# A second table stored by rank from SP's queue, with each node's place carried in the first table

## The chip, the cores and the metric

The kernel runs on one core of a Trainium2 chip. A core has five engines that run at once, each on its own in-order stream: TensorE (PE, matrix products; PEld is its loading of weights), VectorE (DVE), ScalarE (ACT), GpSimd (POOL) and SyncE (SP). Sixteen DMA engines move data between memory and the core's buffers; transfers are issued from the queues of SP, ACT or POOL. The metric is device time of one execution in microseconds, the median of several runs.

## The reference

Two layers of a typed graph transformer over 6250 nodes with 128 features and 100,000 edges, 8 heads of 16 numbers. A node has one of 16 types, an edge one of 32.

```
k, q, v = typed_linear(x, ntype, Wk / Wq / Wv)      # one 128x128 matrix per node type
kT = einsum('nhd,htdo->nhto', k, Watt)              # for every node, all 32 edge types
vT = einsum('nhd,htdo->nhto', v, Wmsg)
kw, m = kT[src, :, etype], vT[src, :, etype]        # one row per edge
a   = einsum('ehd,ehd->eh', kw, q[dst]) * pri[:, etype].T / 4
att = edge_softmax(a, dst)                          # over the edges of one dst
hag = segment_sum(m * att, dst)
h   = silu(typed_linear(hag, ntype, Wa))
h   = h * alpha + x * (1 - alpha)                   # alpha = sigmoid(skip[ntype])
out = layernorm(h) * g + b
```

After two such layers a last linear map is added to the input x and the sum is normalized.

## The kernel before, in words

The kernel forms kT and vT for every node and edge type as a table in device memory: one row of 256 numbers (128 of kT with the softmax scale, 128 of vT) for each pair of node and edge type, 1 KB, about 205 MB per layer. Row number is node × 32 + edge type. An edge then costs one gathered row.

**Ranks.** The nodes are sorted by class of type (four classes of four types) and by degree into 50 blocks of 128; a node's place in this order is its rank, 128 × block + partition. The blocks' numbers of edge slots are fixed ahead (`KB`, 8 to 41, 867 slots in all). `rank_order` (L644 to L927) finds the ranks on VectorE and TensorE: `degrees` compares all destinations with 64 values (L537), then come a histogram (L672 to L686) and a loop over superblocks (L781 to L798) that ends in `rank` at L807. From the ranks it makes lists by place: `start` (first edge), `degr`, `node` and `row2` (the row numbers of a node's table halves, L851). Then it yields "gathers" and issues, on POOL, the gathers of each block's edge list into `ell` (L869: one number node × 32 + edge type for every edge slot) and of its rows of x (L881). `rank_order` is a generator: the table's loop pulls it step by step.

**First table** (L1011 to L1028). It is made in order of type: `inv` says which node stands at each place, `fetch` (L943) gathers its row of x on POOL, `linears0` makes k and v of a window of types, and `table_block` (L287) multiplies each block of 128 nodes by the block matrices of the edge weights, for 16 edge types at a time (`tg` 0 and 1): eight products, copied from PSUM into a tile `st` of 128 × 16 × 256 numbers by ScalarE (L306) or VectorE (L304). `put0` (L1001) scatters `st` into the table on POOL's queue: 16 KB per partition, at the row that `rows1` names. Four `st` tiles exist. 98 such stores make the table; `stage` decides how many steps of ranking go beside each half.

**First edge pass** (`edges(0)`, L1103). The 50 blocks are taken in 15 superblocks of three or four. For each edge slot POOL gathers 128 rows (L1274), one for each node of the block, by the column of `ell`, into a ring `kvr` of 50 slots. For every six to eight slots VectorE multiplies the first half of the rows by q (L1286) and sums by head (L1290); when a block is complete, `finished` computes its softmax (exp on ScalarE, L1170), weighs the second halves (L1189) and adds them up (L1200, L1205), which frees the slots. A slot is gathered into again only when its block's sums are done.

**Nodes and second table.** When a superblock is complete, `nodes` (L1357) computes Wa, the skip, the norm and the next layer's k, v and q; `pieces_of` (L1478) makes the second table from k and v by `table_block` with three `st` tiles, and `scatter` (L1483) stores each tile, three steps late, on POOL's queue, to the row that `row2` names: 100 such stores, between the gathers. The second table thus has the same row numbers as the first, and `ell` serves both passes. Its first gather waits for all of these stores (L1277 to L1284).

**Second edge pass.** It is the same loop over the second table; `nodes` ends in the output rows, scattered on POOL (L1517).

**What orders the work.** POOL's instructions are in the order in which the program writes them (a manual schedule). Those of the other engines are ordered by a planner that models their times and takes what is ready in the order of the program. `tick` and `spread` decide how many steps of `nodes` and `pieces_of` are written for each edge slot. SP's queue carries the loads of rows by rank (`hr`, L1074), of types (`ntb`, L1066) and of q (L1099), and the stores of `hrd` (L1401) and `qrd` (L1452); each waits in order until its buffer is free or its data is there.

Of the kernel before, what the change touches and what calls it, by code (L numbers as in the profile page):

```python
# [18 lines left out]
P = 128  # L19
# [100 lines left out]
def kernel(  # L120
# [60 lines left out]
    tabs = [dram.tile([NP * RT, 2 * D], F32, name=f"tab{l}") for l in range(L)]  # L181
    kvs = dram.tile([PAD, 1], I32, name="kvs")
# [104 lines left out]
    def table_block(pool, ps_pool, kT, vT, i, share, bufs, store, w=1):  # L287


        for tg in range(TG):  # L290
            tt = slice(tg * 16, (tg + 1) * 16)
            st = pool.tile([P, 16, 2 * D], F32, name="st", bufs=bufs)
            for half, (yT, bd) in enumerate(((kT, bdk), (vT, bdv))):
                for hp in range(0, HP, w):
                    pt = ps_pool.tile([P, w, SB * P], F32, name="tb").rearrange(
                        "p b (t c) -> p b t c", t=16)
                    for b in range(w):
                        s = slice((hp + b) * 2 * HS, (hp + b + 1) * 2 * HS)
                        nc.tensor.matmul(pt[:, b], yT[s, i * P:(i + 1) * P], bd[s, tt, :],  # L299
                                         start=True, stop=True)  # L300
                    c0 = half * D + hp * 2 * HS
                    to = st[:, :, c0:c0 + w * 2 * HS].rearrange("p t (b c) -> p b t c", b=w)
                    if hp in share:
                        nc.vector.tensor_copy(to, pt)  # L304
                    else:
                        nc.scalar.copy(to, pt)  # L306
                yield
            store(tg, st)
# [333 lines left out]
    with tc.manual_schedule(engines={mybir.EngineType.Pool}):  # L642

        def rank_order():  # L644
# [162 lines left out]
            nc.vector.tensor_tensor(rank, rank, none, op=ALU.add)  # L807
            ranki = pp.tile([P, NT], I32, name="ranki")
# [202 lines left out]
        got, stage = [], ""  # L1011
        for _ in linears0(got, 0):
            pass
        for t in range(TY):
            b0, _, b1 = spans(t)
            beside = linears0(got, t + 1) if t + 1 < TY else iter(())
            for b in range(b0, b1):
                def store(tg, st, b=b):
                    put0(st, tg, b)
                    fetch(min(b + AHEAD, fetched[0] + 1))  # L1020
                share = (1,) if stage in ("gathers", "done") else ()
                for half, _ in enumerate(table_block(tp, tnb, *got[t], b - b0, share, STB0, store)):
# [11 lines left out]
    def arm(fast):  # L1034
# [9 lines left out]
        if fast:  # L1044
            kvr = npl.tile([P, SLOTS, 2 * D], F32, name="kv")
# [57 lines left out]
        def edges(l):  # L1103
# [50 lines left out]
            def finished(s, i, chunks, kvt, used, a, pair, sums, den):  # L1154
# [74 lines left out]
            for s, (i0, k, types) in enumerate(sbs):  # L1229
# [6 lines left out]
                for i in range(k):  # L1236
# [24 lines left out]
                    for j0, j1 in chunks:  # L1261
# [10 lines left out]
                        for j in range(j0, j1):  # L1272
                            at = KO[b] + j
                            get = nc.gpsimd.indirect_dma_start(  # L1274
                                out=kv[:, j - j0, :], out_offset=None, in_=tabs[l][:],
                                in_offset=bass.IndirectOffsetOnAxis(ap=ell[:, at:at + 1], axis=0))
# [10 lines left out]
                            kk, kk, q.unsqueeze(1).to_broadcast([P, c, D]), op=ALU.mult)  # L1287
                        for r in range(c):
# [189 lines left out]
        def pieces_of(i0, k, kT, vT, share):  # L1478
# [4 lines left out]
            def scatter(tg, st, b):  # L1483
                put = nc.gpsimd.indirect_dma_start(  # L1484
# [200 lines left out]
```

## Time and profile before

| | |
|---|---|
| median of 3 runs | 3683.18 us (3673.71 to 3688.72) |
| profiled execution | 3703.66 us, span 3701.5 us |
| busy: PE, DVE, ACT, POOL | 1811.8, 1953.0, 1018.8, 2150.0 us |
| granted clock of PE, mean | 0.641 |
| moved | 691.11 MB, mean 187 GB/s |

| stage | us from the start |
|---|---|
| loads and order by type | 0 to 61 |
| first table | 61 to 656 |
| first edge pass, nodes, second table | 656 to 2306 |
| second edge pass, output | 2306 to 3701 |

A page of the profile shows the busy time of each engine, the span in 40 slices (each digit a busy share in tenths), the DMA queues, and groups of instructions by line: busy time and mean duration in ns, and after the bar the time for which the engine stood idle just before them, with what ended the waits. A line Lnnn is a line of the kernel. The engine of a wait is the one that waited; behind the arrow stands what it waited for. "Issue" is time in which nothing was waited for that the profile shows.

### The profile page before, as it was taken

The page shows a single profiled execution, that of the slowest core. Times are in us where ns is not written, and L with a number is a line of the kernel's source. Part 1 is how long each engine was busy: PE and PEld are TensorE (multiplying, and loading weights), DVE is VectorE, ACT ScalarE, POOL GpSimd, SP SyncE. Part 2 cuts the span into 40 slices and gives each one's busy share as a digit, 9 for nine tenths or more (in the row PEclk, how much of TensorE's full clock was granted, in tenths as well). Part 3 has the DMA queues.
Part 4 walks back from the last instruction along what each step waited for, and adds up shares of the span by engine and source line. Part 5 has one row for each costly group of instructions (what it writes and reads, how often), then busy time and mean ns, then how long its engine had stood idle before and what let it go on. Part 6 is the DMA issues. An engine that isn't in the chain of part 4 may idle for free. (4 is left out here: it accounts for less than half of the span.)

```text
span 3701.5 us, 22085 instructions
## 1 busy us (share of the span) xinstructions
PE 1811.8 (49%) x5612; PEld 822.8 (22%) x5612; DVE 1953.0 (53%) x4025; ACT 1018.8 (28%) x1677; POOL 2150.0 (58%) x2213
## 2 busy tenths in 40 slices
PE   3898998115555687658677675002120122112112
PEld 1344445002222232222222222001010111101011
DVE  8665231356355665457456633445655447455645
ACT  2675565002331244213332353001100111011111
POOL 2224663674676566666665652765667566666653
PEclk9789675557666776667678677555555555555555
DMA  6797999634655477546764677333333333333321
GB/s 181 309 385 319 399 403 403 161 99 147 218 188 195 140 269 268 176 148 210 268 220 165 241 284 304 107 96 91 95 92 107 86 89 102 92 99 94 91 82 43
DMA packets 194484, 691.11 MB, mean 187 GB/s; under 512 B 55469, under 2 KB 106032, under 8 KB 169298
## 3 DMA queue, kind: packets, MB, share of 16 engines
q0 software_dynamic: 119120, 651.15, 49.7%
q1 hardware_dynamic: 58838, 31.29, 3.2%
q10 hardware_dynamic: 16384, 7.11, 0.9%
q8 instruction: 48, 0.79, 0.1%
q14 instruction: 94, 0.77, 0.1%
HBM read 264.91 MB, written 429.48 MB: 188 GB/s over the span
## 5 line engine op out<-in xcount | busy, mean ns | idle before, releaser
L1274 POOL DMA_INDIRECT kv<-tab,ell x1734 | 1722.7, 993 | 769.2 <-issue 481.5
L306 ACT COPY st<-tb 128x512 f32<-128x512 f32 (+1 forms) x1064 | 726.1, 756 | 510.5 <-PE tb L299 255.0
L284 PE MATMUL nb<-ident,hag 128*128 128x128 f32 x100 | 26.1, 400 | 743.9 <-issue 212.5
L299 PE MATMUL tb<-bdv,kvT 32*128 32x512 f32 x800 | 275.7, 834 | 77.2 <-ACT st L306 66.2
L1484 POOL DMA_INDIRECT tab<-st,row x100 | 106.5, 1065 | 345.3 <-ACT st L306 288.5
L299 PE MATMUL tb<-bdv,vT 32*128 32x512 f32 x784 | 291.9, 868 | 24.4 <-ACT st L306 14.2
L299 PE MATMUL tb<-bdk,kvT 32*128 32x512 f32 x800 | 267.7, 824 | 67.5 <-ACT st L306 60.6
L1286 DVE TENSOR_TENSOR kv<-kv,q 128x896 f32<-128x896 f32 (+4 forms) x135 | 136.3, 1011 | 288.8 <-DMA kv<-tab,ell 260.4
L1290 DVE TENSOR_REDUCE a<-kv 128x48 f32<-128x768 f32 (+4 forms) x269 | 269.8, 1004 | 32.7 <-remote 23.2
L278 PE MATMUL nb<-xm,wa 128*128 128x384 f32 (+1 forms) x384 | 228.9, 758 | 117.5 <-DVE xm L269 79.3
L269 DVE SCALAR_TENSOR_TENSOR xm<-ntb,nb 128x384 f32<-128x384 bf16 (+1 forms) x336 | 184.4, 592 | 169.3 <-PE nb L284 50.6
L299 PE MATMUL tb<-bdk,kT 32*128 32x512 f32 x784 | 257.2, 865 | 0.9 <-issue 0.8
L1002 POOL DMA_INDIRECT tab<-st,rows x98 | 103.7, 1058 | 240.2 <-ACT st L306 195.1
L1286 DVE TENSOR_TENSOR kv<-kv,tb 128x768 f32<-128x768 f32 (+4 forms) x134 | 135.2, 1010 | 157.7 <-DMA kv<-tab,ell 130.7
L284 PE MATMUL nb<-ident,hs 128*128 128x128 f32 x100 | 37.8, 460 | 367.1 <-DVE hs L1395 165.1
L304 DVE COPY st<-tb 128x512 f32<-128x512 f32 (+1 forms) x120 | 89.1, 744 | 199.8 <-PE tb L299 141.1
L284 PEld LDWEIGHTS nb<-ident,hag 128*128 128x128 f32 x100 | 15.9, 198 | 762.5 <-issue 726.1
L278 PE MATMUL nb<-xm,wq 128*128 128x384 f32 (+1 forms) x192 | 106.7, 721 | 118.3 <-DVE m L1165 80.9
L1417 PE MATMUL nb<-xm,wkqv 128*128 128x384 f32 (+1 forms) x288 | 133.3, 617 | 51.0 <-DVE xm L269 32.6
L1200 DVE TENSOR_TENSOR tb<-kv,tb 128x512 f32<-128x512 f32 (+3 forms) x211 | 121.2, 574 | 69.5 <-remote 46.7
L278 PEld LDWEIGHTS nb<-xm,wa 128*128 128x128 f32 x384 | 98.7, 274 | 244.3 <-issue 113.4
L1436 PE MATMUL nb<-xm,wkqv 128*128 128x384 f32 (+1 forms) x288 | 132.3, 619 | 11.6 <-DVE xm L269 9.8
(314 smaller groups left out, 2745.4 us busy)
## 6 DMA issues: line engine op xcount, KB each, us to landing
kv<-tab,ell POOLq DMA_INDIRECT x1734
hr<-xrd SPq DMA_DIRECT2D x30, 192.0 KB
hr<-xrd SPq DMA_DIRECT2D x15, 256.0 KB
xrd<-xr POOLq DMA_DIRECT2D x11, 256.0 KB
ntb<-typed SPq DMA_DIRECT2D x20, 96.0 KB
hrd<-hs SPq DMA_DIRECT2D x10, 192.0 KB
qrd<-q SPq DMA_DIRECT2D x10, 192.0 KB
q<-qrd SPq DMA_DIRECT2D x10, 192.0 KB
```

Of the source, the lines that this page charges most:

```text
L269: nc.vector.scalar_tensor_tensor(xm[:, :n], ntb[:, :n], float(t), hT[:, :n], op0=ALU.is_equal, op1=ALU.mult)
L278: nc.tensor.matmul(ps[:, :n], w[:, t, :], xm[:, :n], start=(t == types[0]), stop=(t == types[-1]))
L299: nc.tensor.matmul(pt[:, b], yT[s, i * P:(i + 1) * P], bd[s, tt, :], start=True, stop=True)
L306: nc.scalar.copy(to, pt)
L1002: put = nc.gpsimd.indirect_dma_start(out=tabs[0].rearrange("(n t) c -> n (t c)", t=16), out_offset=bass.IndirectOffsetOnAxis(ap=rows1[:, t ...
L1200: nc.vector.tensor_tensor(acc[:, :n], v, acc[:, :n], op=ALU.add)
L1274: get = nc.gpsimd.indirect_dma_start(out=kv[:, j - j0, :], out_offset=None, in_=tabs[l][:], in_offset=bass.IndirectOffsetOnAxis(ap=ell[:, ...
L1286: nc.vector.tensor_tensor(kk, kk, q.unsqueeze(1).to_broadcast([P, c, D]), op=ALU.mult)
L1290: nc.vector.tensor_reduce(a[:, j0:j1, :], kk.rearrange("p k (h d) -> p k h d", h=H), axis=AX.X, op=ALU.add)
L1417: nc.tensor.matmul(outs[j][:, :n], wkqv[:, j, t, :], xm[:, :n], start=(t == types[0]), stop=(t == types[-1]))
L1436: nc.tensor.matmul(ps[:, :n], wkqv[:, j, t, :], xm[:, :n], start=(t == types[0]), stop=(t == types[-1]))
L1484: put = nc.gpsimd.indirect_dma_start(out=tabs[1].rearrange("(n t) c -> n (t c)", t=16), out_offset=bass.IndirectOffsetOnAxis(ap=row2[:, tg ...
```

## The change

The second table is laid out by rank: row number rank × 32 + edge type. Its stores have fixed places, so they are plain DMAs, issued by SP. For the second pass `ell` must hold rank × 32 + edge type. This number is put as a 257th word into each row of the first table, so that the gather of the first pass brings it along, and VectorE copies it (with a conversion to integers) over the entry of `ell` that has been used. For that a node's rank must be known when its rows of the first table are stored: the ranks are stored to memory by SP and fetched by POOL, for each block of 128 nodes in the order of types, four blocks ahead; and `rank_order` is run up to `rank` before the loop of the first table begins.

Rows of the first table are 1028 bytes; the ring's slots are 257 words wide in both passes. The rest of `rank_order` goes beside the first table as before.

```diff
+    W0 = 2 * D + 1
+    tab0 = dram.tile([NP * RT, W0], F32, name="tab_first")
+    tab1 = dram.tile([NR * RT, 2 * D], F32, name="tab_second")
+    ranks = dram.tile([NP, 1], F32, name="ranks")
...
-    def table_block(pool, ps_pool, kT, vT, i, share, bufs, store, w=1):
+    def table_block(pool, ps_pool, kT, vT, i, share, bufs, store, w=1, cols=2 * D):
...
-            st = pool.tile([P, 16, 2 * D], F32, name="st", bufs=bufs)
+            st = pool.tile([P, 16, cols], F32, name="st", bufs=bufs)
...
             nc.vector.tensor_tensor(rank, rank, none, op=ALU.add)
+            scaled = pp.tile([P, NT], F32, name="scaled")
+            nc.vector.tensor_scalar(scaled, rank, float(RT), None, op0=ALU.mult)
+            rk_ps = pps.tile([NT, P], F32, name="ps")
+            nc.tensor.transpose(rk_ps, scaled, ident)
+            rkr = pp.tile([NT, P], F32, name="rkr")
+            nc.vector.tensor_copy(rkr, rk_ps)
+            nc.sync.dma_start(ranks.rearrange("(i p) c -> i (p c)", p=P), rkr)
+            yield "ranked"
...
+        ranked = pp.tile([P, NT], F32, name="ranked")
+        asked = [0]
+
+        def ask(end):
+
+            while asked[0] < min(end, NT):
+                g = asked[0]
+                nc.gpsimd.indirect_dma_start(
+                    out=ranked[:, g:g + 1], out_offset=None, in_=ranks[:],
+                    in_offset=bass.IndirectOffsetOnAxis(ap=inv[:, g:g + 1], axis=0))
+                asked[0] += 1
 
         def put0(st, tg, b):
+            nc.vector.tensor_scalar(st[:, :, 2 * D], colf[:, tg * 16:(tg + 1) * 16],
+                                    ranked[:, b:b + 1], None, op0=ALU.add)
             put = nc.gpsimd.indirect_dma_start(
-                out=tabs[0].rearrange("(n t) c -> n (t c)", t=16),
+                out=tab0.rearrange("(n t) c -> n (t c)", t=16),
...
+        while stage != "ranked":
+            stage = next(ranking)
+        ask(4)
         for t in range(TY):
...
                 def store(tg, st, b=b):
                     put0(st, tg, b)
+                    if tg:
+                        ask(asked[0] + 1)
                     fetch(min(b + AHEAD, fetched[0] + 1))
...
-            kvr = npl.tile([P, SLOTS, 2 * D], F32, name="kv")
+            kvr = npl.tile([P, SLOTS, W0], F32, name="kv")
...
-                        v = kvt[j][:, :, D:]
+                        v = kvt[j][:, :, D:2 * D]
...
-                                out=kv[:, j - j0, :], out_offset=None, in_=tabs[l][:],
-                                in_offset=bass.IndirectOffsetOnAxis(ap=ell[:, at:at + 1], axis=0))
+                                out=kv[:, j - j0, :2 * D if l else W0], out_offset=None,
+                                in_=(tab1 if l else tab0)[:], in_offset=bass.IndirectOffsetOnAxis(ap=ell[:, at:at + 1], axis=0))
...
+                        if l == 0:
+                            nc.vector.tensor_copy(ell[:, KO[b] + j0:KO[b] + j1], kv[:, :, 2 * D])
...
             def scatter(tg, st, b):
-                put = nc.gpsimd.indirect_dma_start(
+                if fast:
+                    puts.append(nc.sync.dma_start(
+                        tab1.rearrange("(n g t) c -> g n (t c)", g=TG, t=16)[
+                            tg, b * P:(b + 1) * P, :], st.rearrange("p t c -> p (t c)")))
+                    return
+                nc.gpsimd.indirect_dma_start(
...
-                if fast:
-                    for other in puts:
-                        tc.declare_no_dep(put.ins, other.ins, reason="rows of other nodes")
-                    puts.append(put)
```

More of the change, by code (lines that the diff above doesn't have):

```diff
@@ L1019, in store @@
                     put0(st, tg, b)
+                    if tg:
+                        ask(asked[0] + 1)
                     fetch(min(b + AHEAD, fetched[0] + 1))
                 share = (1,) if stage in ("gathers", "done") else ()
-                for half, _ in enumerate(table_block(tp, tnb, *got[t], b - b0, share, STB0, store)):
+                for half, _ in enumerate(table_block(tp, tnb, *got[t], b - b0, share, STB0, store,
+                                                         cols=W0)):
                     next(beside, None)
```

## The prediction

> **What bounds the kernel now.** I read the page's slices first, then stretches of the span, then the groups of each stretch, then single waits. The slices show three stages: seven slices with DMA at 6 to 9 tenths (first table), then a long middle in which no engine is full, then a flat end.
>
> ```profile
> POOL 2224663674676566666665652765667566666653
> DMA  6797999634655477546764677333333333333321
> ```
>
> The stretches (columns: busy us and instructions of PE, PEld, DVE, ACT and POOL, granted clock, DMA share, GB/s) give each stage its limit. From 61 to 350 us the ranks are computed beside the first table and DMA reaches 0.79; from 350 to 645 us it is full at 402 GB/s. In the first edge pass (656 to 2306 us) PE is busy 1015 of 1650 us, POOL 1006, DVE 884: nobody is full. The second (2306 to 3640 us) has the same gathers without tables.
>
> ```profile
> 61.00:350.00 289.00, 246.40 (x1147) 119.81 (x1146) 195.13 (x534) 183.97 (x362) 92.98 (x98) 0.80 0.79 326
> 350.00:645.00 295.00, 271.76 (x878) 141.22 (x876) 78.86 (x127) 175.42 (x338) 166.67 (x180) 0.66 1.00 402
> 656.00:2306.00 1650.00, 1014.79 (x2860) 404.80 (x2860) 884.26 (x1642) 500.73 (x666) 1005.77 (x967) 0.69 0.60 205
> 2306.00:3640.00 1334.00, 240.60 (x586) 133.98 (x586) 719.44 (x1505) 138.12 (x276) 867.37 (x910) 0.53 0.33 95
> ```
>
> POOL's groups within the first pass explain it: 899.3 + 306.6 + 106.5 + 345.3 = 1657.7 us, the whole stretch. POOL never rests; it gathers, pays about 0.3 us between gathers ("issue"), or stands before a scatter of the second table until ScalarE has copied its tile.
>
> ```profile
> L1274 POOL DMA_INDIRECT kv<-tab,ell x867 | 899.3, 1037 | 306.6 <-issue 240.3 <-DVE acc L1189 18.3 <-DMA tab<-st,rows 17.2
> L1484 POOL DMA_INDIRECT tab<-st,row x100 | 106.5, 1065 | 345.3 <-ACT st L306 288.5 <-issue 18.6 <-DVE st L304 12.4
> ```
>
> In the second pass the same group waits longer, though no scatter is there: 462.6 − 241.3 = 221.3 us are waits for a free slot of the ring of gathered rows, which VectorE frees.
>
> ```profile
> L1274 POOL DMA_INDIRECT kv<-tab,ell x867 | 823.4, 950 | 462.6 <-issue 241.3 <-DVE v L1334 61.8 <-DVE tb L1189 44.8
> ```
>
> Two single waits on POOL: the first scatter holds the gathers behind it for 31.81 us, and the last scatters end in a wait for landing before pass two.
>
> ```profile
> 849.94 1.01 POOL L1274 DMA_INDIRECT kv<-tab,ell  x1 [4.59 <-DVE kv L1286]
> 882.76 1.02 POOL L1484 DMA_INDIRECT tab<-st,row  x1 [31.81 <-ACT st L306]
> 884.08 0.97 POOL L1274 DMA_INDIRECT kv<-tab,ell  x1 [0.30 <-issue]
> ...
> 2306.36 1.00 POOL L1274 DMA_INDIRECT kv<-tab,ell  x1 [9.62 <-DMA tab<-st,row]
> ```
>
> VectorE in the first pass waits 288.8 us for gathered rows, so POOL's standing is felt:
>
> ```profile
> L1286 DVE TENSOR_TENSOR kv<-kv,q 128x896 f32<-128x896 f32 (+4 forms) x135 | 136.3, 1011 | 288.8 <-DMA kv<-tab,ell 260.4 <-issue 28.2
> ```
>
> **Ranks ahead of the first table: a loss, about 112 us.** Today the first store of table one is issued at 61.07 us and the first gather at 656.19. After the change POOL's order has four fetches of ranks before the first store, and they need the finished ranks. Ranking starts with L516 near 44 us. VectorE's instructions of lines 470 to 807 sum to 165.7 us in the trace (64 compares of 963 ns are 61.6 of it). In between it stands for TensorE, today 27 us (L548 15.8, L672 4.9, L565 4.1, L476 and L483 2.6) with table work in TensorE's way; alone I take half, 13: 44 + 166 + 13 = 223 us (L807 ends at 266 today). A transpose, a copy, a store by SP and a fetch by POOL follow. Issue alone is 0.4 + 1.25 us, and the 18 us from the last store's issue at 638.02 to the first gather, which hold the landing of three queued stores, bound it above; I take 6, near the small end, since little moves. First store: 229 us. Four tiles of the table are built by then. The stores are 98 × 128 × 16,448 bytes = 206.3 MB; with some 8 MB of x rows beside them at 402 GB/s that is 533 us: 762, and some 6 us of landing: first gather at 768, against 656. Bounds: no round trips and stores alone, 210 + 513 + 6 = 729 (+73); ranking that ends as late as today, 266 + 6 + 533 + 6 = 811 (+155). I take 112, since the row of the full stretch is the very stage that remains.
>
> The parts beside it: 49 rank fetches of POOL at 1.25 us (as the fetches of L947 at 0.99 with 0.30 between) are 61 us; POOL has 295 − 167 − 180 × 0.3 = 74 us free in the 295 full us, so 134 in 533, and they are hidden; if not, they are 61. 98 additions on VectorE of 128x16 (279 ns for that size at L873) are 27 us beside 79 of 295 busy: hidden, and four tiles of slack cover a late one. SP's queue is passed by the rank store alone there and is idle from 44.56 to 314 us.
>
> **Scatters leave POOL: a gain, about 152 us.** Removed from POOL in pass one: 106.5 us of scatter and 345.3 us before them. What is left is 899.3 + 240.3 = 1139.6 us of gathers, plus the tail from the last gather (about 2228) to 2306, 78 us, which stays: the last tables must still be made and land. Between these stands K, POOL's waits for free slots. Today K hides behind the scatter waits (306.6 − 240.3 = 66 us, lower bound). The upper bound is what keeps the stretch as it is: 1650 − 1139.6 − 78 = 432. The nearest row is pass two, 221 us with the same 867 gathers, the same ring and no scatter. There VectorE is busy 719 us, in pass one 884 and 24 more: the word beside each row is copied to the index table in about 134 casts of some 0.18 us (L543). Scaled, 221 × 908 / 719 = 280. So pass one takes 1139.6 + 280 + 78 = 1498, a gain of 152. The net is K − 320: **the break-even lies at K = 320 us.**
>
> New on SP: 100 stores of 2 MB (0.36 us of issue each by SP's own rows), in order with loads of hr and ntb and the stores of hrd and qrd. SP waits for ScalarE's copies there; behind it stand loads that today are issued a superblock ahead (SP stood 176 us at one hr load without harm). Behind a late load, in turn, a store holds one of three table tiles, 2 × 6.6 us of PE work. Bounds 0 and about 100 us (15 superblocks by those 6.6 us); I take 0, since SP's waits are prefetches, and leave the 100 to the range.
>
> The gathered row grows from 1024 to 1028 bytes and its slot's stride too. Gathers alone keep DMA at 0.37 (2350 to 2450 us), so even a doubling does not fill it; it is priced 0, at most 134 chunks × 0.3 us = 40 us of later arrival, and below nothing by a byte count 0.4% higher it cannot go. Stores move to another queue, so a gather may pass a 5 us store: from 0 to −40 us by the same 134 chunks; the two cancel. Pass two keeps its 1334 us, give or take 10.
>
> Sum on the profiled execution: 3703.66 + 112 − 152 = 3664 us. It stands 20.5 us above the median of the runs shown, so I forecast **3643 us**.
>
> **Two rules of the Trainium skill.** "DMA: Bandwidth & Descriptors", section "Issuing engines are not separate DMA queues", says all issuers share the same 16 engines and another issuer saves only issue time. By that alone the gain would be 106.5 + 18.6 = 125 us and the forecast 3670; the trace's wait of 288.5 us for ScalarE is no transfer, so I expect more. The same page, "How a descriptor splits into AXI transactions", speaks against the longer row: 1028 bytes off a 256-byte boundary need five transactions in place of four. As an estimate that lifts 0.37 to 0.46, still no bound; the sum would stay.
>
> **Rivals.** Slower: the stall moves. TensorE, ScalarE and VectorE are chained (ScalarE waits 173 us at L1170 for VectorE, PE 257 for ScalarE's copies), and the table's tiles came late because of that chain, not of POOL. The ring holds 50 slots, two to three blocks of 14 to 25, so POOL soon waits for VectorE instead. K = 432 gives 3683 + 112 = 3795; it decides from K = 338 on. For it: pass two stalls 221 us with a quarter of the PE work. Against: VectorE waits 289 us for rows.
>
> Much faster: everything follows POOL. K stays at 66, pass one takes 1284 us, 3683 + 112 − 366 = 3429. For it: 656 to 850 us, where 142 gathers run almost unbroken. Against: no tables are made there, and PE's 1015 us would have to fit into 1284 at clock 0.69.
>
> The change does not do what it says: the ranks are no real delay, because copies are built ahead. Four tiles are four stores, 21 us: 3622 at most in favour. Or SP becomes what POOL was: with 100 us, 3743.
>
> **How the numbers follow.** A difference below 0.5% (18 us) is no change here. Forecast (K 190 to 302): 0.36. Much faster: 0.10. Near break-even (K 302 to 338): 0.12. Slower, by K beyond 338 or by SP: 0.42. Faster 0.46, same 0.12, slower 0.42. The likeliest case alone spans 3553 to 3665. Eight in ten: from K = 137 (3500) to K = 432 with some SP loss or later ranks (3805).
>
> **What would show it.** Right: first gather near 768 us; no POOL scatter in the middle; L1274 in pass one with 200 to 300 us beyond issue; pass one near 1500; VectorE's wait for rows well below 289; pass two 1334. Wrong: a wait of POOL at L1274 for VectorE above 340 us, SP waiting for ScalarE while PE waits for hr or ntb, ScalarE waiting for the landing of tab1 stores, first gather beyond 800, or DMA at 1.0 in pass one.

## The result, and the profile after

The changed kernel takes **3915.35 us** (median; 3904.72 to 3916.68), the kernel before on the same chip 3684.99 us (3673.71 to 3688.72). The ratio is **1.062, 95% interval 1.059 to 1.065**: 6.2% slower, where 3643 us and a gain of 1.1% were forecast. The time lies above the top of the range, 3805.

The page's slices of the changed kernel: GpSimd starts later, and toward the end of the first edge pass there is a new slice (2342 to 2439 us) in which it does nothing, while DMA stands at 8 tenths.

```profile
POOL 0056663257666674476545630275676566766662
DMA  4079999953465555665556448732333233333331
```

The stretches (columns as before: busy us and instructions of PE, PEld, DVE, ACT and POOL, granted clock, DMA share, GB/s) are the first table, the first pass up to the first gather of the second, and the second pass:

```profile
205.00:785.00 580.00, 536.53 (x1692) 259.12 (x1692) 195.57 (x436) 321.87 (x608) 299.48 (x325) 0.70 0.93 375
785.00:2510.00 1725.00, 947.09 (x2860) 384.74 (x2860) 878.55 (x1777) 500.16 (x666) 944.05 (x868) 0.69 0.58 200
2510.00:3840.00 1330.00, 235.54 (x582) 131.36 (x583) 716.61 (x1484) 133.59 (x268) 870.86 (x911) 0.53 0.33 95
```

The profiled execution is 201.4 us longer (3902.9 against 3701.5). The first gather comes 128.7 us later (784.87 against 656.19), the first pass takes 75 us more (1725.1 against 1650.2), the rest 2 us less. So the ranks cost 129 us where 112 were forecast, within the bounds, and **the first pass, which should have gained 152 us, lost 75**, although GpSimd's 100 scatters and the 345 us of waits before them are gone.

GpSimd's groups, first in the first pass, then in the second (count, busy, mean ns of one, idle before it):

```profile
L1305 POOL DMA_INDIRECT kv<-tab_first,ell x867 | 944.1, 1089 | 575.5 <-issue 240.5 <-DVE acc L1220 120.1 <-DVE kv L1220 92.4
...
L1305 POOL DMA_INDIRECT kv<-tab_second,ell x867 | 825.8, 953 | 656.8 <-issue 238.7 <-DMA tab_second<-st 217.8 <-DVE v L1367 47.0
```

The waits for slots are now long: 120.1 and 92.4 us behind VectorE's weighting of the rows (L1220). And the second pass opens with a wait of 217.8 us. In GpSimd's order of time, the wait for the ranks, the first store of the first table, the last gather of pass one and the first of pass two:

```profile
194.03 1.05 POOL L1019 DMA_INDIRECT ranked<-ranks,inv  x1 [145.82 <-DMA ranks<-rkr]
...
205.30 1.02 POOL L1027 DMA_INDIRECT tab_first<-st,rows  x1 [0.17 <-issue]
...
2291.22 0.95 POOL L1305 DMA_INDIRECT kv<-tab_first,ell  x1 [0.30 <-issue]
2509.93 0.95 POOL L1305 DMA_INDIRECT kv<-tab_second,ell  x1 [217.76 <-DMA tab_second<-st]
```

Before, the last gather and the first of pass two lay 85 us apart, and 88 of the 100 stores of the second table had been issued by the last gather. After, it is 219 us and 69 stores.

What VectorE stands at has changed its name. Its groups of the first pass, the product of the gathered rows with the queries and the new cast:

```profile
L1317 DVE TENSOR_TENSOR kv<-kv,q 128x896 f32<-128x896 f32 (+4 forms) x135 | 134.9, 1009 | 165.1 <-DMA kv<-tab_first,ell 85.1 <-issue 55.2 <-ACT q L1115 24.5
...
L1320 DVE CAST ell<-kv 128x7 int32<-128x7 f32 (+4 forms) x135 | 25.3, 187 | 332.9 <-DMA kv<-tab_first,ell 292.9 <-issue 40.0
```

The casts are busy 25.3 us and have 332.9 us of idle time ahead of them. A cast needs the gathered rows and nothing else; a product needs the query too. Left to itself the planner puts casts of several coming tiles ahead of other work. Some 40 us of VectorE's order show what follows:

```profile
1501.36 0.21 DVE L1320 CAST ell<-kv 128x6 int32<-128x6 f32 x1
1504.10 0.17 DVE L1320 CAST ell<-kv 128x6 int32<-128x6 f32 x1 [2.52 <-DMA kv<-tab_first,ell]
...
1509.39 0.22 DVE L1320 CAST ell<-kv 128x6 int32<-128x6 f32 x1 [4.95 <-DMA kv<-tab_first,ell]
1516.42 0.19 DVE L1320 CAST ell<-kv 128x5 int32<-128x5 f32 x1 [6.80 <-DMA kv<-tab_first,ell]
...
1531.23 0.17 DVE L1320 CAST ell<-kv 128x6 int32<-128x6 f32 x1 [7.34 <-DMA kv<-tab_first,ell]
1538.07 0.17 DVE L1320 CAST ell<-kv 128x6 int32<-128x6 f32 x1 [6.68 <-DMA kv<-tab_first,ell]
1540.30 1.95 DVE L273 SCALAR_TENSOR_TENSOR xm<-ntb,nb 128x384 f32<-128x384 bf16 x4 [2.05 <-remote]
```

Not one product is among them: the products wait for the next query, the query needs masked inputs (xm, L273), and the masks stand on VectorE *behind* the casts, each of which waits for its gather. TensorE pays:

```profile
1540.99 4.33 PE L282 MATMUL nb<-xm,wq 128*128 128x384 f32 x7 [20.42 <-DVE xm L273]
```

TensorE's waits for masks at this line within the first pass (total us, times, longest), before and after:

```profile
PE nb L278 <- DVE xm L269: 79.8, 22, 12.6
...
PE nb L282 <- DVE xm L273: 260.8, 19, 78.7
```

The longest, 78.7 us, stands near the start of the pass and has a counterpart before (80.9 us, which the trace puts down to L1165). Without it the rise is from 80 to 182 us.

From here two theories were put against each other. A: the casts planned ahead of the masks are the loss. B: GpSimd without scatters just runs ahead of TensorE, and the stall moves to the end of the pass, whatever VectorE's order is. A third, C, blames the landing of the stores on SyncE's queue.

### The profile page after: what moved, and what is told of

Same layout as the page of the kernel before. It is cut to its first block, busy times and chain, and to the rows that moved or that the text cites. A ratio compares the mean times of both kernels' runs of the same rounds, so it can differ in the third digit from the quotient of the medians.

```text
span 3902.9 us, 22359 instructions
## 1 busy us (share of the span) xinstructions
PE 1817.5 (47%) x5613; PEld 833.7 (21%) x5613; DVE 2003.2 (51%) x4328; ACT 993.2 (25%) x1609; POOL 2135.3 (55%) x2162
## 5 line engine op out<-in xcount | busy, mean ns | idle before, releaser
L1305 POOL DMA_INDIRECT kv<-tab_first,ell x867 | 944.1, 1089 | 575.5 <-issue 240.5
L1305 POOL DMA_INDIRECT kv<-tab_second,ell x867 | 825.8, 953 | 656.8 <-issue 238.7
L310 ACT COPY st<-tb 128x512 f32<-128x512 f32 (+1 forms) x996 | 700.3, 768 | 561.0 <-PE tb L303 318.5
L288 PE MATMUL nb<-ident,hag 128*128 128x128 f32 x100 | 25.2, 389 | 746.4 <-issue 232.6
L303 PE MATMUL tb<-bdv,vT 32*128 32x512 f32 x784 | 337.9, 891 | 12.6 <-ACT st L310 6.7
L303 PE MATMUL tb<-bdk,kT 32*128 32x512 f32 x784 | 328.2, 906 | 10.9 <-DVE st L308 5.1
L273 DVE SCALAR_TENSOR_TENSOR xm<-ntb,nb 128x384 f32<-128x384 bf16 (+1 forms) x336 | 183.1, 591 | 195.3 <-PE nb L288 93.9
L303 PE MATMUL tb<-bdv,kvT 32*128 32x512 f32 x800 | 242.5, 800 | 74.9 <-ACT st L310 38.1
L308 DVE COPY st<-tb 128x512 f32<-128x512 f32 (+1 forms) x188 | 135.4, 723 | 254.3 <-PE tb L303 185.3
L1317 DVE TENSOR_TENSOR kv<-kv,q 128x896 f32<-128x896 f32 (+4 forms) x135 | 134.9, 1009 | 165.1 <-DMA kv<-tab_first,ell 85.1
L1027 POOL DMA_INDIRECT tab_first<-st,rows x98 | 99.1, 1011 | 194.3 <-ACT st L310 174.4
L1320 DVE CAST ell<-kv 128x7 int32<-128x7 f32 (+4 forms) x135 | 25.3, 187 | 332.9 <-DMA kv<-tab_first,ell 292.9
L1450 PE MATMUL nb<-xm,wkqv 128*128 128x384 f32 (+1 forms) x288 | 124.8, 583 | 58.6 <-DVE xm L273 34.6
L303 PEld LDWEIGHTS tb<-bdk,kT 32*128 32x128 f32 x784 | 124.6, 253 | 119.0 <-ACT st L310 39.4
```

Of the source, the lines that this page charges most:

```text
L273: nc.vector.scalar_tensor_tensor(xm[:, :n], ntb[:, :n], float(t), hT[:, :n], op0=ALU.is_equal, op1=ALU.mult)
L288: nc.tensor.transpose(tr[:, i * P:(i + 1) * P], src_of(i), ident)
L1027: put = nc.gpsimd.indirect_dma_start(out=tab0.rearrange("(n t) c -> n (t c)", t=16), out_offset=bass.IndirectOffsetOnAxis(ap=rows1[:, tg, ...
L1305: get = nc.gpsimd.indirect_dma_start(out=kv[:, j - j0, :2 * D if l else W0], out_offset=None, in_=(tab1 if l else tab0)[:], in_offset=bass ...
L1317: nc.vector.tensor_tensor(kk, kk, q.unsqueeze(1).to_broadcast([P, c, D]), op=ALU.mult)
L1450: nc.tensor.matmul(outs[j][:, :n], wkqv[:, j, t, :], xm[:, :n], start=(t == types[0]), stop=(t == types[-1]))
```

## The experiments

The first set (the next four runs) ran on one chip, where the kernel before took 3343.42 us, the second set on another, 3341.82 us; the third set ran on a chip where it took 3688.35 us, close to the first comparison's. The traces of the kernel before are of the first comparison alone, so on the quicker chips passes are compared between runs. Every ratio is to the kernel before on its own chip. "Tail" is the time from the last gather of pass one to the first of pass two; the stores of the second table that were issued by that last gather are counted in the trace.

**1. The casts behind their products.**

```diff
-                        nc.vector.tensor_tensor(
+                        times = nc.vector.tensor_tensor(
                             kk, kk, q.unsqueeze(1).to_broadcast([P, c, D]), op=ALU.mult)
                         if l == 0:
-                            nc.vector.tensor_copy(ell[:, KO[b] + j0:KO[b] + j1], kv[:, :, 2 * D])
+                            cast = nc.vector.tensor_copy(ell[:, KO[b] + j0:KO[b] + j1], kv[:, :, 2 * D])
+                            tc.add_manual_dep(cast.ins, times.ins.name,
+                                mybir.DependencyInfo(mybir.DependencyClass.NoSync,
+                                                     mybir.DependencyReason.DATA),
+                                reason="behind the product")
```

> The changed kernel with one dependency more: each cast (L1320 there) stands on VectorE behind the product of its own tile, not ahead of it in the planner's order. Nothing else differs. Theory A (the casts, which need only the gathered rows, are planned ahead of the masks that the query projections need; VectorE stands at them for gathers, TensorE then for the masks, and the tables of the second table fall late): the 293 us that VectorE waits at the cast are gone from it, the wait of TensorE for the masks falls from 261 us to under 100, the wait of GpSimd for the last stores of the second table falls from 218 us to 80 to 130, its other waits for slots in pass one from 323 us to 200 to 280, and the time is 3720 to 3830 us. Rival B (GpSimd, which no longer scatters, simply runs ahead of TensorE, and the stall moves to the end of pass one whatever VectorE's order is): the waits change their names, the tail stays over 180 us, and the time is 3890 to 3940 us. Rival C (the landing of the stores on SyncE's queue is what is late): the same time as B, with SyncE or the landings, not TensorE, behind the tail.

Measured: 3400.17 us, **ratio 1.018 [1.015, 1.021]**. The groups of pass one, VectorE's and GpSimd's:

```profile
L1317 DVE TENSOR_TENSOR kv<-kv,q 128x896 f32<-128x896 f32 (+4 forms) x135 | 136.7, 1014 | 322.9 <-DMA kv<-tab_first,ell 250.3 <-issue 50.4 <-ACT q L1115 22.2
L1320 DVE CAST ell<-kv 128x7 int32<-128x7 f32 (+4 forms) x135 | 23.7, 176 | 0.0
...
L1305 POOL DMA_INDIRECT kv<-tab_first,ell x867 | 956.6, 1103 | 310.5 <-issue 223.1 <-DVE acc L1220 17.1 <-DMA kv<-tab_first,ell 13.4
```

The wait went from the cast back to the product, and GpSimd's waits for slots are 75 us (310.5 − 223.1, less the 12.3 us of the first gather's wait for the first table). So A holds for the time. It does not hold for the tail: that is still 176 us (A said 80 to 130), with 72 stores issued by the last gather. There B is nearer (over 180). Nor does it hold for TensorE's wait for the masks, which is 250.5 us (A said under 100), 163.7 without the long one at the start.

**2. No casts at all.**

```diff
-                        if l == 0:
-                            nc.vector.tensor_copy(ell[:, KO[b] + j0:KO[b] + j1], kv[:, :, 2 * D])
```

> The changed kernel without its casts: the lists keep the node numbers, so that pass two gathers other rows of the second table than the reference's; everything else is there, the word in the rows and the additions too. Theory A: as with the casts held behind their products and about 25 us of VectorE's time less: 3700 to 3820 us, the tail 80 to 130 us. Rival B and rival C: 3870 to 3930 us, since the casts by themselves are only 25 us of VectorE.

Measured: 3394.07 us, ratio 1.016 [1.013, 1.019], tail 173 us. Casts that stand behind their products cost nothing that can be measured (3400.17 − 3394.07 = 6 us; the intervals overlap).

**3. Only the ranks ahead.** In `rank_order` a `yield "ranked"` behind the line that ends `rank`, and before the loop of the first table:

```diff
+        while stage != "ranked":
+            stage = next(ranking)
```

> The kernel before with one part of the change: the stages that make the ranks run ahead of the first table. No word, no second table by rank, no cast; GpSimd still scatters. All theories: the first gather at 745 to 785 us against 656 us, pass one and two as before, so 3770 to 3815 us. If the ranks' work was in the way of pass one where it stood, part of this comes back and the time is under 3750 us.

Measured: 3475.61 us, **ratio 1.040 [1.037, 1.043]**, somewhat above the expected 1.023 to 1.036 (3770 to 3815 us of 3685). The first gather is at 788 us, the first pass takes 1477 us. The stretches show where the time lies:

```profile
61.00:260.00 199.00, 127.21 (x495) 62.89 (x494) 148.08 (x417) 35.35 (x65) 12.48 (x12) 0.56 0.14 55
260.00:770.00 510.00, 469.57 (x1537) 241.40 (x1537) 160.81 (x308) 295.56 (x568) 243.42 (x266) 0.65 0.96 391
```

DMA is used at 0.14 while the ranks are made, then it is full. In the whole change the ranks cost a little less on such a chip: its first gather was at 759 us in runs 1 and 5, against 654 us in run 4, where no ranks are ahead: 105 us.

**4. Only the second table by rank, stored by SyncE.**

```diff
+    tab1 = dram.tile([NR * RT, 2 * D], F32, name="tab_second")
...
-                                out=kv[:, j - j0, :], out_offset=None, in_=tabs[l][:],
+                                out=kv[:, j - j0, :], out_offset=None, in_=(tab1 if l else tabs[0])[:],
...
+                if fast:
+                    puts.append(nc.sync.dma_start(
+                        tab1.rearrange("(n g t) c -> g n (t c)", g=TG, t=16)[
+                            tg, b * P:(b + 1) * P, :], st.rearrange("p t c -> p (t c)")))
+                    return
```

> The kernel before with another part of the change alone: the second table is stored in rank order by plain transfers on SyncE's queue, and GpSimd no longer scatters. No ranks ahead, no word, no additions, no casts; the lists keep the node numbers, so that pass two gathers other rows of the second table than the reference's. Theory A: the gain that was forecast for the scatters, 152 us, comes here nearly whole: 3510 to 3580 us, GpSimd's waits for slots in pass one 230 to 300 us, the tail 80 to 130 us. Rival B (the stall moves to the tail whatever VectorE does): 3640 to 3720 us with a tail over 150 us. Rival C (SyncE's queue makes the stores late): also 3640 us or more, with SyncE's wait for landings or GpSimd's wait for them long while TensorE has finished the tables.

Measured: 3291.71 us, **ratio 0.985 [0.982, 0.988]**, a gain of 52 us where A expected about 150. GpSimd in pass one and at its end:

```profile
L1275 POOL DMA_INDIRECT kv<-tab,ell x867 | 965.5, 1114 | 311.5 <-issue 220.4 <-DMA kv<-tab,ell 19.2 <-DMA tab<-st,rows 17.3
L1275 POOL DMA_INDIRECT kv<-tab_second,ell x1 | 0.9, 940 | 173.7 <-DMA tab_second<-st 173.7
```

The gathers run almost unbroken: 1259 us from first to last, where the same pass with scatters, behind ranks made ahead, needs 1393 (run 3). But the tail takes 175 us in place of 85. B is nearer here: two thirds of what the gathers gain against run 3 are given back at the end, when 27 stores are still to come and DMA is busy at 0.88.

**5. The changed kernel on a chip of this kind.** Without an edit, so that runs 1 and 2 have something to be compared with.

> The changed kernel as it is, beside the others of this set on one chip. With the casts behind their products it was 1.018 of before on another chip than the first comparison's. Theory A (the casts that are planned ahead of the masks cost what lies between): 1.05 to 1.07 of before here too. If the first comparison's chip made the difference: 1.01 to 1.03.

Measured: 3604.17 us, **ratio 1.0785 [1.076, 1.081]**. The pass takes 1638 us against 1430 in run 1. TensorE's wait for the masks within the pass (total us, times, longest), here:

```profile
PE nb L282 <- DVE xm L273: 366.5, 24, 78.0
```

and in run 1, with the casts behind:

```profile
PE nb L282 <- DVE xm L273: 250.5, 18, 86.8
```

The one dependency of run 1 is worth (1.0785 − 1.018) × 3342 = **202 us**. The two passes differ by 208 us: 165 in the gathers (1419 against 1254) and 43 in the tail (219 against 176). GpSimd's waits for slots are 250 us here and 75 in run 1. In VectorE's order in the trace, 156 of the 312 masks between the first and the last product of pass one have one to nine casts of products still to come ahead of them; in run 1 none has. The rest adds up: 3343 + 105 for the ranks − 52 of run 4 = 3396 us, and run 1 took 3400.

**6. The tables sooner**, on top of run 1.

```diff
-                    spread(pieces, gen, 8 * sbs[s][1] + 4, (1.0 if s + 4 < len(sbs) else 0.6) * slots(min(s + 2, len(sbs) - 1)))
+                    spread(pieces, gen, 8 * sbs[s][1] + 4, (0.6 if s + 4 < len(sbs) else 0.4) * slots(min(s + 2, len(sbs) - 1)))
```

> The changed kernel with the casts behind their products and the pieces of the second table written into the order sooner: spread over 0.6 of two superblocks' slots and 0.4 of them for the last, where it was 1.0 and 0.6. Theory D (the tail of 176 us after the last gather of pass one is there because TensorE reaches the tables some 13 stores later than the gathers, which no scatter holds back any more; TensorE has time, it stands 250 us at the masks): stores issued by the last gather rise from 73 to over 80, the tail falls to 100 to 140 us and the time to 0.985 to 1.01 of before. Rival E (TensorE is the bound of pass one, and what is put sooner delays the queries behind it by as much): tail shorter, gathers later, 1.01 to 1.03 of before.

Measured: 3447.65 us, ratio 1.031 [1.029, 1.033]: slower than run 1. 75 stores were issued by the last gather, not over 80, and the tail grew to 203 us. Theory D's remedy fails; what is written sooner delays the queries behind it (VectorE's wait for ScalarE's copy of q rose from 22 to 59 us), which is what rival E said. E's shorter tail did not come either.

**7. The same plain stores, issued by GpSimd** at the place of the scatters: run 4 with one word changed.

```diff
-                    puts.append(nc.sync.dma_start(
+                    puts.append(nc.gpsimd.dma_start(
```

> The kernel before with the second table stored in rank order by plain transfers, as in the run with SyncE's queue, but issued by GpSimd at the place of the scatters in its order; pass two gathers other rows than the reference's. Theory D (the scatter's place in GpSimd's order is what kept gathers and tables in step): GpSimd waits for ScalarE's copies 100 us and more again, the tail falls back from 175 us to 80 to 95, gathers take 1370 to 1420 us where they took 1259, and the time is 0.985 to 1.005 of before. Rival C (SyncE's queue is late): the tail falls and the gathers stay fast: 0.94 to 0.96.

Measured: 3303.61 us, ratio 0.988 [0.985, 0.990], the same as run 4 within the intervals.

```profile
L1275 POOL DMA_INDIRECT kv<-tab,ell x867 | 924.1, 1066 | 297.4 <-issue 218.8 <-DMA tab<-st,rows 17.7 <-DMA kv<-tab,ell 11.5
L1486 POOL DMA_DIRECT2D tab_second<-st x100 | 57.6, 577 | 172.6 <-ACT st L307 135.0 <-DVE st L305 13.5 <-DVE hs L1396 7.4
```

The waits for ScalarE are back, the tail is 85 us, 88 stores are issued by the last gather, as D said; the gathers take 1359 us, just under D's 1370 to 1420. **In this pair the wait at a store in GpSimd's order is no loss of its own. It holds the gathers in step with the tables; without it the same time is spent at the end.** SyncE's queue is not what is late (rival C expected 0.94 to 0.96).

**8. The casts alone**, in the kernel before.

```diff
+                        if l == 0:
+                            word = ep.tile([P, MOST], I32, name="word")
+                            nc.vector.tensor_copy(word[:, :c], kv[:, :, 2 * D - 1])
```

> The kernel before with the cast alone: behind the product of each tile of pass one, in the order of the code, a cast of one word a row into a small tile of integers that nothing reads; the planner is free to put it ahead, as in the changed kernel. Theory A: 1.02 to 1.05 of before, VectorE's wait for gathers split between cast and product, TensorE's wait for the masks up. Rival F (hoisted casts cost only where GpSimd no longer scatters, since the scatters hold everything in step anyway): 1.00 to 1.015.

Measured: 3362.61 us, ratio 1.006 [1.004, 1.009]. Rival F is right and A, as it was put, wrong: the same 135 casts cost 21 us here. VectorE's group for them in pass one:

```profile
L1290 DVE CAST word<-kv 128x7 int32<-128x7 f32 (+4 forms) x135 | 23.1, 171 | 50.2 <-DMA kv<-tab,ell 50.2
```

50.2 us of idle time stand before them, not 332.9, and in VectorE's order only 4 of the 324 masks between the first and the last product have casts ahead. So it needs both: the casts *and* stores that are out of GpSimd's order. This is theory G: the stores in GpSimd's written order hold the gathers back in the planner's reckoning too, so it takes rows to come late and keeps casts behind; with the stores on SyncE it takes them to come early. The orders are counted in the traces; what the planner reckons is inferred from them.

**9. The changed kernel with its stores on GpSimd**, the edit of run 7 and no other.

> The changed kernel with one word changed: the second table's plain stores are issued by GpSimd, at the place in its order where the scatters stood, and not by SyncE. The casts are free, ranks ahead and word stay. Theory G (with the stores out of GpSimd's order the planner takes the gathers to be early, and puts 1 to 9 casts ahead of 156 of the 312 masks of pass one; with the stores in it, ahead of 4): the casts cost next to nothing, and what stays is the ranks' 104 us less the 41 us that the plain stores on GpSimd brought, so 1.015 to 1.035 of before. If the casts cost by themselves: 1.06 and more.

Measured: 3723.99 us, **ratio 1.011 [1.007, 1.015]**, against 1.062 for the changed kernel on a chip with the same time before: one word removes five sixths of the loss. The planner may still put the casts where it likes, and they do no harm, since only 4 of 324 masks have casts ahead:

```profile
L1320 DVE CAST ell<-kv 128x7 int32<-128x7 f32 (+4 forms) x135 | 22.5, 167 | 49.1 <-DMA kv<-tab_first,ell 27.8 <-issue 21.2
```

The pass takes 1539 us, 111 less than the 1650 of before, with a tail of 87; the first gather is at 784 us, 128 later than before. GpSimd's groups of the pass:

```profile
L1305 POOL DMA_INDIRECT kv<-tab_first,ell x867 | 898.1, 1036 | 323.3 <-issue 238.0 <-DVE acc L1220 24.1 <-DMA tab_first<-st,rows 12.6
L1518 POOL DMA_DIRECT2D tab_second<-st x100 | 57.6, 577 | 260.8 <-ACT st L310 213.9 <-DVE st L308 13.5 <-ACT hb L1407 8.9
```

The waits for slots are 73 us, and what the stores take is 318 us with their waits, where the scatters took 452. This run gives back the order too, not the casts' place alone, so it does not price the casts by themselves on this chip.

**10. Stores by SyncE and casts**, which the planner may put where it likes, no ranks ahead, no word: runs 4 and 8 together.

> The kernel before with the second table stored by SyncE's queue (pass two gathers other rows than the reference's) and the free casts into a tile that nothing reads; no ranks ahead, no word. Theory G: the 200 us of the casts come here in full, 0.985 + 0.06 = 1.035 to 1.055 of before, where each part alone gave 0.985 and 1.006. If the cost came of the lists that the casts write, or of the longer rows: 0.985 to 1.00.

Measured: 3775.17 us, ratio 1.025 [1.021, 1.030]. Apart they gave 0.985 and 1.006, on the quicker chips. That is below the expected 1.035 to 1.055, but clearly above 1: the lists, the word and the ranks are not needed for the loss. The pass takes 1722 us, as in the changed kernel (1725), and the group is the one of the changed kernel; again 156 of 312 masks have casts ahead:

```profile
L1291 DVE CAST word<-kv 128x7 int32<-128x7 f32 (+4 forms) x135 | 25.3, 188 | 339.1 <-DMA kv<-tab,ell 297.1 <-issue 41.9
```

**11. The scatters later**, in the kernel before.

```diff
-                    late.append([3, (tg, st, b)])
+                    late.append([6, (tg, st, b)])
```

> The kernel before, its scatters put six half-steps behind their tiles in GpSimd's order, not three. What GpSimd waits for ScalarE at the scatters (115 us in such a run) is what theory D says holds gathers and tables in step: the wait falls to 60 us or less, but the tail grows by 20 to 50 us, 0.985 to 1.00 of before. If the waits were a loss by themselves: 0.96 to 0.975.

Measured: 3693.45 us, ratio 1.000 [0.997, 1.004]. GpSimd's wait for ScalarE at the scatters was 232.6 us, against 288.5 in the profile before. The expected numbers were of the quicker chips, but even so the wait fell by a fifth where about a half was expected, and the tail grew from 85 to 100 us, less than the 20 to 50 us expected. No gain, as run 7 would have it; the test is a weak one, since the wait moved little.

**12. Both mends**, runs 1 and 9 together.

> The changed kernel with both mends, the casts behind their products and the stores issued by GpSimd. Theory G: no better than either alone, since each takes away the same stall: 1.015 to 1.03 of before, with a tail of 85 us and the first gather at 759 us, so that what is left is the ranks. If the two mends add: under 1.00, and the change is worth making.

Measured: 3712.99 us, ratio 1.008 [1.005, 1.011], the same as run 9 within the intervals; pass one 1535 us, tail 88. The mends don't add, since little is left for a second one: in run 9 only 4 masks have casts ahead, here none. The first gather was at 787 us, not 759: that figure was of the other chips.

No version of the whole change that was tried beats the kernel before on its chip: the best is 0.8% slower. Both mends together were not run on the quicker chips.

| kernel | chip's before, us | ratio | gathers of pass one, us | tail, us | stores issued by the last gather |
|---|---|---|---|---|---|
| before | 3685 | 1 | 1565 | 85 | 88 |
| changed | 3685 | 1.062 | 1506 | 219 | 69 |
| 9 stores on GpSimd | 3688 | 1.011 | 1452 | 87 | 88 |
| 5 changed | 3342 | 1.0785 | 1419 | 219 | 69 |
| 1 casts behind | 3343 | 1.018 | 1254 | 176 | 72 |
| 4 SyncE stores alone | 3343 | 0.985 | 1259 | 175 | 73 |
| 7 GpSimd stores alone | 3342 | 0.988 | 1359 | 85 | 88 |

## Why the prediction was wrong, point by point

**The ranks ahead: right.** Forecast +112 us (73 to 155), measured +128.7 in the profiled execution. The first store was earlier than forecast (205.3 us, not 229). The sum of 166 us counts durations that overlap in the trace: from 44 to 193 us VectorE is busy 138 us and idle 10. The 98 stores were slower (566 us from first to last, not 533). Two things lie in those 566 us: DMA stood at 0.93 in that stretch, not at 1.00, and the word's addition (L1025), priced as hidden, waited 70.3 us on VectorE for the landing of its tile's earlier store, with copies behind it. How much of the 33 us is this wait was not tried.

**The scatters leave: wrong, and here the forecast fell.** Pass one was to take 899.3 + 240.3 + 280 + 78 = 1498 us. Measured: 944.1 + 240.5 + 323 + 218 = 1725. Of the 227 us between them the tail is 140, the gathers 45 and K 43. Two steps failed: the casts were priced by their duration, and the stores' leaving GpSimd's order was priced as a wait that goes and a tail that stays. The terms and what became of them:

- "134 casts of some 0.18 us" were priced as 24 us of VectorE's time. Their duration was right (25.3 us). What was not asked is *where they stand in VectorE's order*. Ahead of the masks they cost 202 us (run 5 against run 1), through GpSimd's waits for slots (K, 250 against 75 us) and through the tail (219 against 176). With the one word changed that puts both the casts and the stores back into step (run 9), the pass takes 1539 us, 41 more than forecast. This is the step that turned the forecast gain into a loss.
- "The tail of 78 us, which stays" was 85 by the trace (the last gather is at 2221.25 us, not 2228), and it did not stay, even without casts: 175 us in run 4. The prediction took the scatter waits as a pure loss. Run 7 shows that they hold gathers and tables in step. Of 134 us that the gathers gained in run 4 against run 3 (1259 against 1393), 90 came back in the tail.
- The gathers' own 899 us became 944. The row of 1028 bytes is not it: in run 9, with the same rows, one takes 1036 ns, as before (1037). With stores on SyncE it is 1084 to 1114 ns, with 1024-byte rows too (run 4). It is a few long ones: 23 to 32 of the 867 take over 2 us with stores on SyncE, 8 to 12 with stores on GpSimd, and the median is 946 to 949 ns in every trace. Closer gathers on average are not the reason: the changed kernel's are spread over 1506 us, run 9's over 1452. What makes these few long was not separated.
- K, scaled from pass two to 280, was 323 in the changed kernel, just past the break-even of 320. But K was no single quantity. Before the change it was 49 us, not 66 (17.2 us are the first gather's wait for the first table); with the casts behind it was 75 us on a quicker chip (run 1), and in run 9, on a chip like the first, 73. Pass two's 221 us, 212 without the first wait, was no measure of it: the same pass has 43 to 47 us on the quicker chips (below).

**SyncE as a new stall: rightly priced at nothing.** SyncE waited 715 us for ScalarE's copies in the changed kernel, but TensorE's waits in pass one name neither hr nor ntb, and plain stores by SyncE or GpSimd come out alike (runs 4 and 7). The 176 us "at one hr load" of the prediction is a row of five loads; the longest single stand at such a load was 120 us, so that argument was weaker than it looked. But leaving GpSimd's order had a price of another kind, and no row of the profile before shows it: the planner's order of VectorE changed.

**Pass two: right.** 1334 ± 10 us was forecast, and 1330 is the stretch above. The ends of both stretches were set by hand; from the first gather to the last it is 1317 us against 1329, and to the end of the program 1393 against 1395. It was right on a chip like the first; it says nothing of others.

**The rivals.** "The stall moves" had the right sign, at 3795 us. It saw that GpSimd would end up waiting for VectorE (212 us behind L1220 alone), and the 257 us that it read as TensorE's wait for ScalarE's copies are those of its weight loads (the products themselves wait 126.7). But it took a chain of three engines to be the limit, while run 1 shows the same chain run the pass in 1430 us where the changed kernel on a quicker chip needs 1638 (run 5). That its number lies nearer to the result than the forecast is in part luck, since the main loss it did not name. The range ended at 3805 because it priced every loss by waits that existed before. Of the signs named as "wrong", SyncE waiting for copies did appear, harmlessly; the sign that told the cause, a wait of VectorE at the *cast*, was not on the list, although the cast was the one new instruction that reads gathered rows. One sign of "right" came and misled: VectorE's wait at the product fell from 288.8 to 165.1 us, because it had moved to the cast.

**The two rules of the skill.** The Trainium skill's page "DMA: Bandwidth & Descriptors", section "Issuing engines are not separate DMA queues", holds that another issuer saves only the time of issuing. Runs 4 and 7 agree: 0.985 [0.982, 0.988] by SyncE, 0.988 [0.985, 0.990] by GpSimd. By the rule the prediction worked out a gain of 125 us and took 152, because of the 288.5 us of waits for ScalarE. Neither came: with the stores on SyncE and no casts, the whole gain was 52 us (run 4, on a quicker chip). The 111 us of run 9 are no test of the rule, since its stores are still issued by GpSimd. The same page's "How a descriptor splits into AXI transactions" speaks against rows off a 256-byte boundary. GpSimd's time for a gather shows nothing of it: 1036 ns with the longer row (run 9), 1037 with the shorter. The DMA engines' time does. Before, from 665 to 815 us, GpSimd's queue takes 36.6% of 16 engines for 110 gathers, 8.0 us each; in run 9, from 793 to 960 us, 36.5% for 110, 8.9 us each. That is a tenth more, and less than the quarter that the prediction's estimate of five transactions for four allows; the DMA share was 0.44 in both stretches, so it was no bound.

## What to carry to other kernels

An instruction that can run as soon as a transfer lands is not priced by its duration: on an in-order engine, ask what the planner may put it ahead of, and whom that work feeds; tie it behind a neighbour if it is in no hurry. Before a wait is counted as a gain, ask what it keeps in step: if the engine behind it has no slack, the time is spent at the next barrier, here the tail before pass two. And moving an operation out of an order written by hand changes what the planner believes of all the others, so compare the planned orders of the other engines before the times.

## What the runs showed of the hardware that was not expected

The time differs by a tenth from chip to chip. The kernel before takes 3685 us in the first comparison and 3688 in the third set, 3343 and 3342 in the first and second set. The changed kernel's pass two, with the same instructions, takes 1317 us from its first gather to its last in the first comparison and 1147 in run 5. Durations are alike (gathers of pass two 825.8 and 823.1 us in all). The waits differ: beside issue and the first wait, GpSimd stands 656.8 − 238.7 − 217.8 = 200 us in that group in the one, and 43.5 us (490.2 − 228.7 − 218.0) in the other. The granted clock is no sign of it (0.650 and 0.667 over the span), and the order of instructions on VectorE, ScalarE and GpSimd is the same in both traces. One place where it shows is the end of a superblock in pass two: in the first comparison SyncE's next load of hr and VectorE's norm, which both need TensorE's last product, start at 2984.46 us, 6.6 us after that product ends by its record; in run 5 the load follows the product by 0.02 us. Since ends of products are modelled in the trace, TensorE may be later than its records say; that is not shown, and what makes the difference is open. It bears on the case: the K that the prediction scaled from pass two was in good part a property of the chip, and the parts of the change weigh differently on each (stores on GpSimd took 111 us from pass one in run 9, with casts and ranks; run 7 took 33 against run 3).
